# A recurrent kernel whose gaps are filled by hand: 512-column gate groups in even steps, the input product in odd steps, the low-rank layer's products spread out, and the opening in source order

## The chip, the cores and the metric

The kernel runs on one NeuronCore of a Trainium2 chip. The metric is the device time of one execution in microseconds; the kernel before takes 1655.66 us as a median of three runs (1653.91 to 1658.54). One further execution was profiled: it took 1656.13 us, of which the trace shows a span of 1654.2 us from the first instruction to the last.

## What is computed

The input is x of shape 16 x 512 x 512 (batch b, time s, feature) and one condition vector of 512 values for each batch, all fp32. Four residual layers follow one another:

```python
x = x + L0(x, cond)   # L0 comes to x * (1 + gate): gate = sigmoid(silu(cond@W1.T + b1)@W2.T + b2)
x = x + L1(x, cond)   # h_s = tanh(x_s@Wx + b + h_{s-1}@Wh), h_{-1} = cond, 512 steps in a row
x = x + L2(x, cond)   # f, i: sigmoids of x@Wf, x@Wi, divided by f+i+1e-8; candidate x@Wh + b_h;
                      # then a cumulative product and sums along time
x = x + L3(x, cond)   # x @ (base + A_b B_b^T): A_b, B_b of rank 8, made from cond by
                      # LayerNorm, w1, gelu, w2 and a bias
```

Only L1 is a chain through time: step s needs all of step s-1. L2's gates are products of L1's output with three 512 x 512 matrices, and can be formed for any step that is done. L3's factors A_b and B_b depend on the condition alone.

## The kernel before, in words

**Opening (lines 180 to 256).** SP issues the loads in a fixed order: the condition, the vectors, w1, w2, the first block of x, Wx, Wh, the second block. LayerNorm of the condition runs on DVE and is turned on PE (L212). `turned_layer` (L226) forms L0's gate in two products (L231, `ps_hq` and `ps_g`), each with a DVE transpose (L240), a bias (L241) and a sigmoid (L243). `gated` (L164) then makes x1 = x * (gate + 2) of the first two blocks (L166). `begin` (L427) opens a PSUM bank for a later block: ScalarE copies the bias into it (L443), and for the first two blocks PE first writes zeros with small products (L435). In program order these L435 products stand behind `ps_g`, ahead of the first product with Wx.

**The recurrent stage (lines 466 to 548).** 64 blocks of 8 steps. All three kinds of product on PE are cut in four tiles of 32 output partitions, one for each j or c, which run side by side in the array; an fp32 product is two instructions of each kind in the trace. I call four such products side by side of 128 moving columns one *unit*. A step is: 4 units of h @ Wh (L328 with `wh_sb`, 32 instructions); then *filler*, which doesn't depend on this step; then ScalarE's tanh in four parts (L508), DVE's four transposes (L509), whose first result lets PE go on with the next step. In steps 4 to 7 of a block DVE adds the finished pair of steps to x1, giving x2 (L514); in steps 0 to 3 it gates a quarter of the block after next (L166).

The filler is dealt out by hand in program order:
- x1 @ Wx of the next block (`inputs`, L328 with `wx_sb`): 16 units for a block, dealt by `SHARE` (L451 to L454), two to a step as a rule.
- L3's products: one weight chunk of 256 KB gives one unit (`factor_part`, L300), in steps 4 to 7 of blocks 0 to 16. `load_factor` (L281) loads two chunks at once in step 6 and two in step 0 of the next block, into four buffers; factor A comes first (r = 0 to 7), then B with its bias rows (L291). `store_factor` (L309) writes the result to memory. The first of these layers ends in a gelu (L279), in four ScalarE instructions with a table load ahead.
- Part of L2's gates made ahead (`early_gate`, L345): products over 256 columns (L364), equal to two units, one in each of six of eight steps from step 64 and one in every step from step 128. Each gate needs four of them. Of three gates in turn (f, i, candidate) ScalarE makes the sigmoids of f and i (L385), DVE sums them (L406), inverts the sum in four pieces (L388), multiplies (L391, L411, L398), and SP stores the parts (L382). A table `jobs` fixes in which step each piece is emitted; `do_jobs` (L524) comes *ahead of* `begin` (L525 to L529) in a step.

All engines run their own instructions in program order here (manual schedule, L460). PSUM's eight banks are six for the blocks' sums (`ps_r`), one for `pg`, one for `pf`.

**The last stage (lines 553 to 656).** For each batch four `gate_unit`s (L562): three groups of products (L568) over the steps that were not made ahead (from `te`, L564: 128 for batches 0 to 11, 192 for 12 to 15), two sigmoids (L583), a chain of eleven or so DVE instructions (L584 to L599, three scans among them), and two additions on GpSimd (L602, L603) that give x3. `load_layer` (L605) fetches A and B and adds A's bias on GpSimd (L614); `make_layer` (L617) forms base + A B^T on PE (L624) and DVE (L627); `last_layer` (L629) is the product with x3 (L634), a ScalarE copy (L638) and the store. It runs one batch late, after the second gate unit of the next batch; for the last batch after the fourth.

## Time and profile before

| | us |
|---|---|
| median of three runs (lowest, highest) | 1655.66 (1653.91, 1658.54) |
| the profiled execution, its span | 1656.13, 1654.2 |
| first tanh (L508) starts | 21.16 |
| first tanh of block 1, of block 8, of block 17, of block 63 | 37.26, 132.09, 266.25, 911.34 |
| first product of the last stage (L568) starts | 924.12 |
| last_layer of batch 13 has been issued, batch 14's third gate unit starts | 1570.70 |
| the last x3 lets PE go on (L634) | 1637.66 |

The page gives each engine's busy time, and PE is busy almost throughout. Since every product's record overlaps the next, that share says little by itself; what counts is the distance from one start to the next. A row of the timeline is: start, time from the first start to the last end of the merged instructions, engine, line, operation, output and inputs, how many were merged; in brackets the idle time of that engine just before, and what ended it. PEld is the load of the stationary operand, which runs ahead of the product. The granted TensorE clock is 0.999 of full in this execution. DMA is busy for 43% of the time from 37 to 132 us, 40% from 132 to 266 and 13% from 266 to 911. The page lists the queue of PE's instructions with 242 packets and 3.96 MB, and the other instruction queue with 72 and 0.59 MB.

### The profile page before, as it was taken

Reading aid. Unit: us, or ns where it says so; the run is one execution under the profiler, and the core shown is the slowest. Engines: PE = TensorE matmul, PEld = TensorE weight load, DVE = VectorE, ACT = ScalarE, POOL = GpSimd, SP = SyncE. Lnnn points to the kernel's source line nnn. Section 1 sums busy time; section 2 is a strip of 40 time slices with the busy share of each in tenths; the row PEclk is TensorE's granted clock in tenths of the full one; section 3 lists DMA queues with packets and bytes.
Section 4 is the critical chain, followed back from the end, with each engine's and each line's share of the span. In section 5 each row is a group of like instructions: output and inputs, shape, how many; then the busy total and the mean of one; then the engine's idle time right before and its main releaser. Section 6 shows DMA issues by size and latency. Waiting matters only on the chain.

```text
span 1654.2 us, 71063 instructions
## 1 busy us (share of the span) xinstructions
PE 1621.6 (98%) x30885; PEld 1193.3 (72%) x30885; DVE 1126.9 (68%) x3589; ACT 428.3 (26%) x2519; POOL 206.3 (12%) x209
## 2 busy tenths in 40 slices
PE   7999999999999999999999999999999999999997
PEld 6888888888888888888888555555555555556563
DVE  3445555555556556555555789888888888988885
ACT  3333333333333333333333111111111111111111
POOL 0000000000000000000000132232323232323331
PEclk9999999999999999999999999999999999999999
DMA  5444431111111111111110110111111111011111
GB/s 184 115 146 123 132 113 52 36 31 36 36 36 36 36 36 37 36 35 34 36 36 24 24 36 26 40 37 34 41 37 41 37 40 40 27 37 47 47 40 56
DMA packets 109130, 85.76 MB, mean 52 GB/s; under 512 B 23296, under 2 KB 87296, under 8 KB 108816
## 3 DMA queue, kind: packets, MB, share of 16 engines
q1 hardware_dynamic: 107712, 81.12, 16.2%
q8 instruction: 242, 3.96, 1.1%
q14 instruction: 72, 0.59, 0.1%
q10 hardware_dynamic: 1104, 0.08, 0.0%
HBM read 54.43 MB, written 26.74 MB: 49 GB/s over the span
## 4 chain that ended last, share of the span: by engine, by line
PE 94%; DVE 3%; issue 1%; ACT 1%; DMA 1%; SPq 0%; POOLq 0%; POOL 0%; DVEq 0%; ACTq 0%
PE pre L328 41%; PE po L634 12%; PE pg L364 11%; PE pf L568 9%; PE pi L568 9%; PE pc L568 9%; PE pl L624 1%; PE pf L300 1%; DVE s L585 1%; DVE h_out L509 1%; ACT a L508 1%; DVE s L593 0%; DMA w_sb<-in_w1T_dram 0%; DVE s L597 0%; DVE i L596 0%
## 5 line engine op out<-in xcount | busy, mean ns | idle before, releaser
L328 PE MATMUL pre<-wh_sb,h_out 128*32 128x128 f32 x16384 | 553.3, 273 | 8.1 <-issue 2.1
L328 PEld LDWEIGHTS pre<-wh_sb,h_out 128*32 128x32 f32 x16384 | 462.4, 110 | 100.6 <-DVE h_out L509 86.2
L509 DVE STREAM_TRANSPOSE h_out<-a 128x32 f32<-128x32 f32 x2048 | 261.9, 185 | 367.2 <-ACT a L508 366.1
L508 ACT ACTIVATE a<-pre 128x32 f32<-128x32 f32 x2048 | 238.0, 203 | 566.6 <-PE pre L328 564.0
L328 PE MATMUL pre<-wx_sb,x 128*32 128x128 f32 x8192 | 325.4, 273 | 0.7 <-issue 0.7
L328 PEld LDWEIGHTS pre<-wx_sb,x 128*32 128x32 f32 x8192 | 240.3, 110 | 6.6 <-ACT pre L443 5.1
L634 PE MATMUL po<-layer,x 128*128 128x512 f32 x480 | 208.8, 593 | 1.1 <-DVE base_sb L627 1.1
L568 PE MATMUL pf<-x,wf_sb 128*128 128x384 f32 (+1 forms) x512 | 170.6, 476 | 3.5 <-ACT f L583 2.6
L634 PEld LDWEIGHTS po<-layer,x 128*128 128x128 f32 x480 | 91.0, 190 | 113.0 <-issue 106.7
L568 PE MATMUL pi<-x,wi_sb 128*128 128x384 f32 (+1 forms) x512 | 168.8, 473 | 0.0
L568 PE MATMUL pc<-x,wc_sb 128*128 128x384 f32 (+1 forms) x512 | 168.8, 473 | 0.0
L585 DVE RECIPROCAL s<-s 128x384 f32<-128x384 f32 (+1 forms) x64 | 157.0, 2453 | 2.2
L568 PEld LDWEIGHTS pf<-x,wf_sb 128*128 128x128 f32 x512 | 95.8, 190 | 76.8 <-issue 16.6
L568 PEld LDWEIGHTS pc<-x,wc_sb 128*128 128x128 f32 x512 | 97.3, 190 | 61.0
L568 PEld LDWEIGHTS pi<-x,wi_sb 128*128 128x128 f32 x512 | 97.3, 190 | 61.0
L602 POOL TENSOR_TENSOR s<-s,f 128x512 f32<-128x512 f32 x64 | 87.0, 1360 | 386.7 <-DVE s L597 374.5
L514 DVE TENSOR_TENSOR x<-x,h_out 128x128 f32<-128x128 f32 x256 | 101.0, 395 | 26.2 <-PE pg L364 3.7
L556 POOL MEMSET zero<- 128x1 f32 x1 | 0.1, 98 | 924.9 <-DMA early<-ei 924.9
L583 ACT ACTIVATE f<-pf,vec_sb 128x384 f32<-128x384 f32 (+1 forms) x64 | 36.4, 568 | 280.3 <-POOL s L602 134.7
L638 ACT COPY osb<-po 128x512 f32<-128x512 f32 x64 | 37.4, 585 | 267.3 <-PE po L634 149.0
L584 DVE SCALAR_TENSOR_TENSOR s<-f,i 128x384 f32<-128x384 f32 (+1 forms) x64 | 35.5, 555 | 95.3 <-ACT i L583 95.3
L364 PE MATMUL pg<-x,wi_sb 128*32 128x256 f32 x1152 | 90.6, 379 | 1.3 <-ACT ef L385 1.3
(84 smaller groups left out, 1338.1 us busy)
## 6 DMA issues: line engine op xcount, KB each, us to landing
xb<-in_xT_dram SPq DMA_DIRECT2D x64, 256.0 KB
w<-in_l3w_dram SPq DMA_DIRECT2D x64, 256.0 KB
out_dram<-osb SPq DMA_DIRECT2D x64, 256.0 KB
early<-ef SPq DMA_DIRECT2D x36, 128.0 KB
early<-ei SPq DMA_DIRECT2D x36, 128.0 KB
f<-early SPq DMA_DIRECT2D x48, 64.0 KB
i<-early SPq DMA_DIRECT2D x48, 64.0 KB
f<-early SPq DMA_DIRECT2D x16, 96.0 KB
```

The costliest lines, as they stand in the source:

```text
L328: nc.tensor.matmul(pre[PLACE[g][0]][j * BP : (j + 1) * BP, PLACE[g][1], :], lhsT, tile_columns(w, j), start=False, stop=False, skip_group_ ...
L364: nc.tensor.matmul(ps[c * BP : (c + 1) * BP, :, :], w[:, k, j * P + c * BP : j * P + (c + 1) * BP], x2[:, k, batches, steps], start=(k == ...
L508: nc.scalar.activation(a[:, at], pre[bank][:, place, at], AF.Tanh)
L509: nc.vector.transpose(turned[:, c, :], a[:, at])
L514: nc.vector.tensor_tensor(x2[:, :, :, at].rearrange("p k b t -> p k t b"), xs[n][:, :, t0 // 2, :, :], turned.rearrange("p k (t b) -> p k ...
L568: nc.tensor.matmul(p[:, te:], w_sb[:, k, j * P : (j + 1) * P], x2[:, k, b, te:], start=(k == 0), stop=(k == KC - 1),)
L583: nc.scalar.activation(gate[:, new], p[:, new], AF.Sigmoid, bias=col(bias, j))
L584: nc.vector.scalar_tensor_tensor(s[:, new], f[:, new], EPS, i[:, new], ALU.add, ALU.add)
L585: nc.vector.reciprocal(s[:, new], s[:, new])
L602: nc.gpsimd.tensor_tensor(s, s, f, ALU.add)
L634: nc.tensor.matmul(po, x3[:, k, at], layer[:, k, :], start=(k == 0), stop=(k == KC - 1))
L638: nc.scalar.copy(osb, po)
```

## The change

Filler is dealt anew. A gate product covers 512 columns (four units at once), over sets of 4 or 8 batches; it stands in steps 0, 2 and 4 of blocks 8 to 16, and 0, 2, 4 and 6 from block 17. x1 @ Wx takes the odd steps, three or four units in each. There are 18 sets of three gates, with as many gate columns in all as before; batches 0 to 7 have 128 steps made ahead, batches 8 to 15 have 192 for two of the four feature groups and 128 for the others (`made_before`). A set's DVE work is cut into 16 pieces, of which one is done in a step, after the `begin` of that step; the f sigmoid is delayed by six steps. In the last block gates stand in steps 0, 2, 3, 4 and 6.

L3's products stand in steps 1, 3, 5, 7 of blocks 1 to 16. A chunk is loaded whenever one was used, three ahead. B's layers come first; A's bias goes through memory (`turn_bias`, block 2) and is added where the factor is made, with four small loads for each layer, and GpSimd's additions in the last stage go. The gelu is one instruction, its bias added on DVE.

In the opening the zeroing of the banks is done by 24 bf16 products placed ahead of everything else on PE, with the bias copies behind them; the LayerNorm turns stand between the two products of L0; the second and third block of x get buffers of their own. At the end, the last batch's layer is made right after batch 14's gates, and the last gate unit's two additions are done on DVE.

The core of the diff:

```diff
-WIDE = 256
-FIRST, MAIN = 64, 128
-SLOTS = (0, 2, 4, 5, 6, 7)
-QUAD = slice(12, 16)
-PARTS = [(QUAD, slice(0, 64))]
-PARTS += [(slice(b, b + 2), slice(0, 128)) for b in range(0, 12, 2)]
-PARTS += [(QUAD, slice(64, 128)), (QUAD, slice(128, 192))]
+WIDE = 512
+FIRST, MAIN = 64 // T, 128 // T + 1
+SETS = [(slice(8, 16), slice(0, 64), j) for j in (0, 1)]
+SETS += [(slice(b, b + 4), slice(0, 128), j) for b in (0, 4) for j in range(KC)]
+SETS += [(slice(b, b + 4), slice(0, 128), j) for b in (8, 12) for j in (2, 3)]
+SETS += [(slice(b, b + 4), slice(64, 192), j) for b in (8, 12) for j in (0, 1)]
+PARTS = [()] * FIRST + [(0, 2, 4)] * (MAIN - FIRST) + [(0, 2, 4, 6)] * (NBLK - MAIN - 1) + [(0, 2, 3, 4, 6)]
...
+    bias_a = dram.tile([R, D], F32, name="bias_a")
...
+    def begin(n, i, blank=None):
+        bank = ps_r.tile([P, G, P], F32, tag=f"pre{i}", name=f"pre_{n}_{i}")
+        n_place = sum(b == i for b, _ in PLACE)
+        if blank is not None:
+            for j in range(KC):
+                nc.tensor.matmul(
+                    bank[j * BP : (j + 1) * BP, :n_place, :],
+                    blank[:, :BP],
+                    blank[:, : n_place * P].rearrange("p (n f) -> p n f", n=n_place),
+                    start=True,
+                    stop=False,
+                    skip_group_check=True,
+                )
+        nc.scalar.copy(
...
         w1_sb = pre.tile([P, KC, D], F32)
         w2_sb = pre.tile([P, KC, D], F32)
         cond_sb = pre.tile([B, D], F32)
+        nc.sync.dma_start(out=cond_sb, in_=cond)
         nc.sync.dma_start(out=condT_sb, in_=chunks(condT))
-        nc.gpsimd.tensor_copy(h0[:, :, B : 2 * B], condT_sb)
-        nc.sync.dma_start(out=cond_sb, in_=cond)
         nc.sync.dma_start(out=vec_sb, in_=vecs)
         nc.sync.dma_start(out=w1_sb, in_=chunks(w1T))
         nc.sync.dma_start(out=w2_sb, in_=chunks(w2T))
-        x0 = load_x(0, pre)
+        x0 = load_x(0, pre, "x0")
         nc.sync.dma_start(out=wx_sb, in_=chunks(wx))
         nc.sync.dma_start(out=wh_sb, in_=chunks(wh))
-        xb = load_x(1)
+        x1 = load_x(1, pre, "x1")
+        xb = load_x(2)
+        for j in range(KC):
+            nc.scalar.dma_start(
+                out=bias_sb[j * BP : (j + 1) * BP],
+                in_=l1b[:, j * BP : (j + 1) * BP]
+                .rearrange("(o c) f -> o c f", o=1)
+                .to_broadcast([BP, KC, BP]),
+            )
+        blank = pre.tile([P, 2 * P], BF16)
+        nc.gpsimd.memset(blank, 0.0)
+        nc.gpsimd.memset(h0, 0.0)
+        nc.gpsimd.tensor_copy(h0[:, :, B : 2 * B], condT_sb)
         make_identity(nc, ident)
+        for tile_ in (aeT, hT3, b2a_raw, *h_out[G - 2 : T - 1]):
+            nc.gpsimd.memset(tile_, 0.0)
...
-        for k in range(KC):
-            ps = ps_pre.tile([P, B], F32, tag="ae", name=f"ae_{k}")
-            nc.tensor.transpose(ps, xhat[:, k * P : (k + 1) * P], ident[:B, :B])
-            nc.vector.tensor_scalar(
-                aeT[:, k, :B], ps, col(C_LNG, k), col(C_LNB, k), ALU.mult, ALU.add
-            )
-        for j in range(KC):
-            nc.scalar.dma_start(
-                out=bias_sb[j * BP : (j + 1) * BP],
-                in_=l1b[:, j * BP : (j + 1) * BP]
-                .rearrange("(o c) f -> o c f", o=1)
-                .to_broadcast([BP, KC, BP]),
-            )
-        nc.scalar.dma_start(out=b2a_raw[:, :, :R], in_=b2a)
-        def turned_layer(src, w_sb, which, name):
+        banks = [[begin(n, i, blank) for i in range(NBANK)] for n in range(2)]
+        def turned_layer(src, w_sb, which, name, between):
...
+        turned = ps_pre.tile([P, KC, B], F32, tag="ae", name="ae")
+        def turn():
+            for k in range(KC):
+                nc.tensor.transpose(turned[:, k, :], xhat[:, k * P : (k + 1) * P], ident[:B, :B])
+        def scale():
+            for k in range(KC):
+                nc.vector.tensor_scalar(
+                    aeT[:, k, :B], turned[:, k, :], col(C_LNG, k), col(C_LNB, k), ALU.mult, ALU.add
+                )
+        z, gate = turned_layer(lambda k: h0[:, k, B:], w1_sb, C_L0B1, "hq", turn)
         hq = pre.tile([P, KC, BP], F32)
         nc.vector.tensor_tensor(hq, z, gate, ALU.mult)
-        _, gate = turned_layer(lambda k: hq[:, k, :], w2_sb, C_L0B2, "g")
+        _, gate = turned_layer(lambda k: hq[:, k, :], w2_sb, C_L0B2, "g", scale)
...
+    LAYERS = [None] + [(which, r) for which in (1, 0) for r in range(R)]
+    AHEAD = 3
+    chunk_sb = []
+    def load_chunk():
+        m = len(chunk_sb)
+        if m == KC * len(LAYERS):
+            return
+        i, k = divmod(m, KC)
+        w = l3w2[LAYERS[i]] if i else l3w1
+        chunk_sb.append(w2pool.tile([P, D], F32, tag="w2", name=f"w2_{i}_{k}", bufs=AHEAD))
+        nc.sync.dma_start(out=chunk_sb[m], in_=w[k * P : (k + 1) * P, :])
...
+        if k == 0:
+            layer_part.ps = ps_p.tile([P, P], F32, tag="pf", name=f"pf_{i}")
+            if i:
+                which, r = LAYERS[i]
+                layer_part.bias = w2pool.tile([P, P], F32, tag="b2", name=f"b2_{i}", bufs=2)
+                for j in range(KC):
+                    nc.sync.dma_start(
+                        out=layer_part.bias[j * BP : (j + 1) * BP, :],
+                        in_=(bias_a, b2b)[which][r : r + 1, j * P : (j + 1) * P].to_broadcast([BP, P]),
...
+        load_chunk()
+    def end_layer(i):
+        ps = layer_part.ps
         got = w2pool.tile([P, P], F32, tag="got", name=f"got_{i}")
-        if which:
-            nc.vector.tensor_tensor(got, ps, bias, ALU.add)
+        if i:
+            which, r = LAYERS[i]
+            nc.vector.tensor_tensor(got, ps, layer_part.bias, ALU.add)
+            for j in range(KC):
+                nc.sync.dma_start(
+                    out=factor[which][:, r, j * P : (j + 1) * P], in_=got[j * BP : j * BP + B, :]
+                )
         else:
-            nc.vector.tensor_copy(got, ps)
-        for j in range(KC):
-            nc.sync.dma_start(
-                out=factor[which][:, r, j * P : (j + 1) * P], in_=got[j * BP : j * BP + B, :]
-            )
+            z = got.rearrange("p (c f) -> p c f", c=KC)
+            nc.vector.transpose(z, ps.rearrange("p (c f) -> p c f", c=KC))
+            nc.vector.tensor_tensor(z, z, vector_of(C_L3B1), ALU.add)
+            nc.scalar.activation(hT3[:, :, :B], z[:, :, :B], AF.Gelu)
...
+    timed, urgent, pieces = {}, [], []
+    def do_pieces(step):
+        for jobs in (urgent, pieces):
+            if jobs:
+                jobs.pop(0)()
+                break
+        for job in timed.pop(step, ()):
+            job()
...
+        number, which = divmod(u, 3)
+        batches, steps, j = SETS[number]
+        shape = dict(b=batches.stop - batches.start, t=steps.stop - steps.start)
+        first = number < 2
...
+            pool, tag = ((ps_q, "pg"), (ps_p, "pf"))[0 if first else u % 2]
+            early_gate.ps = pool.tile([P, WIDE], F32, tag=tag, name=f"pg_{u}")
...
+        def end_input_gate():
+            sigmoid(i, C_BI)
+            early_gate.sums = [lambda at=at: total(at) for at in halves]
+            pieces.extend(early_gate.sums)
+            for n in range(8):
+                at = slice(n * WIDE // 8, (n + 1) * WIDE // 8)
+                pieces.append(lambda at=at: invert(at))
+            pieces.extend(lambda at=at: normalize(0, at) for at in halves)
         if which == 0:
-            later(now if single else now + 2, lambda: activate(f, AF.Sigmoid, C_BF))
+            timed.setdefault(step if first else step + 6, []).append(lambda: sigmoid(f, C_BF))
         elif which == 1:
-            later(now, lambda: activate(i, AF.Sigmoid, C_BI))
-            later(now + 1, lambda: nc.vector.scalar_tensor_tensor(s, f, EPS, i, ALU.add, ALU.add))
-            for n in range(4):
-                at = slice(n * WIDE // 4, (n + 1) * WIDE // 4)
-                later(now + 2 + n, lambda at=at: part_of_reciprocal(at))
-            later(now + 6, normalize_f)
-            later(now + 7, lambda: nc.vector.tensor_tensor(i, i, s, ALU.mult))
+            timed.setdefault(step, []).append(end_input_gate)
         else:
-            if first:
-                later(now, lambda: activate(candidate, AF.Identity, C_BH))
-            later(now + (3 if first else 4), times_candidate)
...
+            assert not any(job in pieces for job in early_gate.sums)
+            urgent.extend(lambda at=at: times_candidate(at) for at in halves)
...
-    SHARE[0] = (0, 0), (0, 0), (0, 0), (0, 3), (3, 7), (7, 10), (10, 13), (13, 16)
-    for n in range(FIRST // T, MAIN // T):
-        SHARE[n] = (0, 2), (2, 6), (6, 8), (8, 12), (12, 13), (13, 14), (14, 15), (15, 16)
+    SHARE[0] = (0, 0), (0, 0), (0, 0), (0, 3), (3, 5), (5, 7), (7, 9), (9, 11)
+    SHARE[1] = (0, 0), (0, 0), (0, 3), (3, 5), (5, 8), (8, 10), (10, 14), (14, 16)
+    LATE = {0: (11, 14), 1: (14, 16)}
+    for n in range(FIRST, MAIN):
+        SHARE[n] = (0, 0), (0, 3), (0, 0), (3, 6), (0, 0), (6, 9), (9, 13), (13, 16)
+    for n in range(MAIN, NBLK):
+        SHARE[n] = (0, 0), (0, 4), (0, 0), (4, 8), (0, 0), (8, 12), (0, 0), (12, 16)
+    LAYER_STEPS = [(4, 5, 6, 7)] + [(1, 3, 5, 7)] * (len(LAYERS) - 1)
+    LAYER_STEPS += [()] * (NBLK - len(LAYERS))
...
-            step = n * T + s
-            if step >= MAIN or step >= FIRST and s in SLOTS:
-                early_gate.step = step
-                early_gate(made)
+            if s in LAYER_STEPS[n]:
+                layer_part(n, LAYER_STEPS[n].index(s))
+            if s in PARTS[n]:
+                early_gate(made, n * T + s)
...
-            do_jobs(step)
             if s in BEGINS:
                 if s < T - 1 and 0 < n < NBLK - 1:
                     nxt.append(begin(n + 1, BEGINS[s]))
                 elif s == T - 1 and n + 2 < NBLK:
                     ahead.append(begin(n + 2, BEGINS[s]))
-        if n == 0:
-            finish_first(loaded)
-        elif loaded:
-            store_factor(n - 1, loaded)
+            do_pieces(n * T + s)
+        if n < len(LAYERS):
+            end_layer(n)
...
-    for step in sorted(jobs):
-        do_jobs(step)
+            turn_bias()
+        pre, nxt = nxt, ahead
+    while urgent or pieces:
+        do_pieces(S)
...
-        te = TE if b in range(B)[QUAD] else MAIN
+        te = made_before(b, j)
...
-        nc.gpsimd.tensor_tensor(s, s, f, ALU.add)
-        nc.gpsimd.tensor_tensor(x3[:, j, :], s, x2[:, j, b, :], ALU.add)
+        engine = nc.vector if (b, j) == (B - 1, KC - 1) else nc.gpsimd
+        engine.tensor_tensor(s, s, f, ALU.add)
+        engine.tensor_tensor(x3[:, j, :], s, x2[:, j, b, :], ALU.add)
...
-        for c in range(KC):
-            rows = slice(c * BP, c * BP + R)
-            nc.gpsimd.tensor_tensor(at[rows, :], at[rows, :], b2a_sb[rows, :], ALU.add)
...
-            if j == (1 if end else 2):
-                to = base_sb if end else layer
-                make_layer(b, at, bt, to)
-                made = (b, x3, to)
-        pending = made
+            if j == 2 and not end:
+                make_layer(b, *factors, layer)
+            if j == KC - 1 and b == B - 2:
+                make_layer(B - 1, *load_layer(B - 1), base_sb)
+        pending = b, x3, base_sb if end else layer
```

## What I expect, worked out before the run

> **What bounds the kernel now.** I read the page first, then the timeline of single steps, then the start of the first tanh (L508) of each of the 512 steps, whose distances show every disturbance. An undisturbed step comes in two lengths. Past 266 us it is PE's own work:
>
> ```profile
> 302.78 0.62 PE L328 MATMUL pre<-wx_sb,x 128*32 128x128 f32 x16
> 303.03 0.47 ACT L508 ACTIVATE a<-pre 128x32 f32<-128x32 f32 x4 [1.28 <-PE pre L328]
> ...
> 303.22 0.61 PE L364 MATMUL pg<-x,wi_sb 128*32 128x256 f32 x8
> 303.26 0.49 DVE L509 STREAM_TRANSPOSE h_out<-a 128x32 f32<-128x32 f32 x4 [0.71 <-ACT a L508]
> ...
> 303.65 1.06 PE L328 MATMUL pre<-wh_sb,h_out 128*32 128x128 f32 x32
> ```
>
> From start to start: 0.44 us for two units of x1 @ Wx, 0.43 for a gate product, and 0.87 for h @ Wh; a step is 1.742 us. With less filler the chain through ScalarE and DVE sets it:
>
> ```profile
> 40.27 0.62 PE L328 MATMUL pre<-wx_sb,x 128*32 128x128 f32 x16
> 40.52 0.47 ACT L508 ACTIVATE a<-pre 128x32 f32<-128x32 f32 x4 [1.18 <-PE pre L328]
> ...
> 41.02 0.81 PEld L328 LDWEIGHTS pre<-wh_sb,h_out 128*32 128x32 f32 x32 [0.40 <-DVE h_out L509]
> ```
>
> PE waits 0.40 for h; tanh to tanh is 1.644. So up to three units of filler are free, and four cost 1.742. Both schedules deal four units almost everywhere: the gain can come only from what disturbs steps, and from the two ends. Two disturbances stand out.
>
> ```profile
> 307.38 0.47 ACT L385 ACTIVATE ei<-pg,vec_sb 128x256 f32<-128x256 f32 x1 [0.40 <-PE pg L364]
> 307.75 0.38 ACT L443 COPY pre<-bias_sb 128x256 f32<-128x256 f32 x1
> 308.18 0.38 PEld L328 LDWEIGHTS pre<-wx_sb,x 128*32 128x32 f32 x16 [0.27 <-ACT pre L443]
> ```
>
> Every third block a sigmoid that must wait for its product stands ahead of the bank's bias copy, and the next step's x1 @ Wx waits for the copy: that step takes 1.945, 0.20 too long.
>
> ```profile
> 152.51 0.61 PE L328 MATMUL pre<-wh_sb,h_out 128*32 128x128 f32 x15
> ...
> 153.59 0.71 PE L328 MATMUL pre<-wh_sb,h_out 128*32 128x128 f32 x17 [0.47 <-issue]
> ```
>
> Here PE stands still amid h @ Wh, with nothing to wait for. Such gaps lie at the 3542nd, 3925th, 4308th, 4819th, 5203rd, 6225th and 6864th product recorded, 383, 383, 511, 384, 1022 and 639 apart: multiples of 128 but for one or two. 128 products and their loads are 256 instructions, and the page has 242 instruction packets of 16 KB for PE's 61,770. So PE waits for its code. It happens only while DMA is 40% busy (to 266 us).
>
> **The change part by part.** *Opening.* In program order PE zeroes the banks behind the gate's second product:
>
> ```profile
> 15.32 3.67 PE L435 MATMUL pre<-ident,h_out 128*32 128x128 f32 x64 [0.44 <-DVE z_g L240]
> ...
> 18.74 1.43 PE L328 MATMUL pre<-wx_sb,x 128*32 128x128 f32 x32
> ...
> 19.97 1.06 PE L328 MATMUL pre<-wh_sb,h_out 128*32 128x128 f32 x32
> ```
>
> Afterwards the 24 small products run while PE waits for w1 (until 8.47). The first gate product, broken up by the turns (8.47 to 11.58), should take what the second takes (1.98): 1.1 us sooner. From there to the gated x takes 5.5 (11.58 to 17.10), so until 16.0, then 1.23 of x1 @ Wx: h @ Wh at 17.2. Wh must have landed: 4.5 MB up to it, at 268 GB/s (DMA view, first 23 us), takes 16.9, no later. But DVE gates block 1 ahead of the first transposes, and that load landed at 17.94; 0.90 later, at 18.84, the transposes begin. Step 1 then starts at 19.1 instead of 21.73: **2.6** (between 1.5 and 3.2).
>
> *Block 0.* From the second tanh to the ninth took 14.33. Afterwards two steps of four units, five of three: 2 x 1.742 + 5 x 1.644 = 11.7. The gelu made its tanh 1.35 late (table load 1.28, four gelus 0.90). With one gelu (0.24 by the 64-wide shape's nearest row, tanh's 0.20): tanh's end and copy to 0.7, load to 2.0, gelu to 2.2, where 1.64 was due: 0.6 late. **2.0**.
>
> *Blocks 1 to 7* took 94.83 against 56 x 1.644 = 92.06: 2.8 of gaps. Chunks now come one in two steps, not two at once. *Blocks 8 to 16* took 134.16 against 72 x 1.742 = 125.4: 8.7, of which 1.7 is a sigmoid that waits for the store of `ef` (the next use is now eight steps behind the store), 0.65 three steps of five units (none now), 0.9 the copy, and 5.5 gaps. In these blocks the Trainium skill speaks against me: "Runtime: NRT & Kernel Launch", Instruction fetch mechanics, says that code is fetched ahead in 16 KiB blocks and crossing into the next is mostly hidden. By it smoother loads would give nothing, and I would keep 2.8 + 5.5. The gap rows, 0.5 to 0.9 us each, say otherwise. Instructions also fall, from 58 to 55 pairs of load and product a step. Against that stand steps 5 to 7 of blocks 8 to 16, three of 64 pairs in a row. I take 1.6 left of 2.8 and 3.5 of 5.5 (the new table load for sigmoid included): **1.2** (-1 to 2.7) and **5.5** (134.16 - 125.2 - 3.5; 1 to 8.5).
>
> *Blocks 17 to 62* took 645.09. 128 columns take 109 ns and 256 take 216 (1.742 less twelve short ones, halved), so 512 should take 429; two steps are 24 x 0.109 + 2 x 0.429 = 3.478, 1.739 each. The copy now precedes the sigmoid, and its bank is first used a step later. 368 x 1.739 + 0.9 (other gaps, kept) = 640.7: **4.4** (3 to 5.3). The wide sigmoid has no row: 320 and 384 columns take 0.53 and 0.58, so 0.69; twice the 256 would be 0.95. The i sigmoid can start 0.87 after tanh and the next tanh is due at 1.74: cover 0.18, and 0.1 of slack in the chain. At nothing; at most 18 x 0.1. DVE's piece (0.54 at most) ends at 1.80 after tanh where its transposes are due at 1.97. Without that cover each late piece would cost 0.1.
>
> *Last block*: five steps get four units instead of two: 5 x 0.09 = **-0.4**. Nine DVE pieces stand behind the loop instead of five, some 2 us; ScalarE's f in the last stage waited for the last store until 928.14, now until 930.2. PE needs that bank at 931.9: covered.
>
> *SP's queue* gets eight more layers with four bias loads (0.7 each by b2b's row: 2.8 in a 13 us block) and is moved past the x loads; SP waits for DVE over 275 us there, and a chunk is asked for six steps ahead. At nothing; else PE would wait for chunks in odd steps. GpSimd's L614 (35 us) leaves an engine that PE never waits for before 1637.
>
> *Last stage.* PE runs without a gap until batch 13's last layer is done (1570.70). A 384-wide unit costs 1.257 more than a 320-wide ((45.96 - 40.93) / 4, batch to batch). By then 14 narrow units lie behind instead of 10: 5.0 sooner. DVE is the bound after that, without idle time from 1579.23 to 1634.93, then GpSimd:
>
> ```profile
> 1636.35 1.26 POOL L603 TENSOR_TENSOR x<-s,x 128x512 f32<-128x512 f32 x1
> 1637.66 0.50 PEld L634 LDWEIGHTS po<-base_sb,x 128*128 128x128 f32 x2 [4.68 <-POOL x L603]
> ```
>
> Four of its six units become wide, 0.57 each (reciprocal 2.15 to 2.55, the rest 0.17): +2.3. Two additions on DVE (0.69 each) replace 2.66: -1.3. The layer's four additions only change place. So 5.0 - 1.0 = **4.0** (2 to 4.5).
>
> **Sum.** 2.6 + 2.0 + 1.2 + 5.5 + 4.4 - 0.4 + 4.0 = 19.3. The profiled execution (1656.13: span 1654.2 and 1.9 around it) becomes 1636.8; it lay 0.5 above the median, which I leave inside the rounding: **1637**.
>
> **The rivals.** *The code gaps stay* (20%): the three dense steps give as much trouble as the bursts did. The 3.2 won on gaps (1.2 + 2.0) are lost, and the dense run adds 0.3 in each of nine blocks: 1637 + 3.2 + 2.7 = 1643. For it: a step of 64 pairs uses up its 128 instructions in 1.74 us, two of them a packet in 3.5, and packets started 3.4 to 5.2 us apart here. Against: they begin where DMA bursts. *The gaps go entirely* (12%): 1.6 + 3.5 more, 1632. *The change doesn't do what it says* (4%): copies and sigmoids meet elsewhere and the opening stays bound by loads; only the tail and the five-unit steps win: about 1651. *Slower* (4%): four 512-wide products side by side don't run at their columns' rate. Place L364's successor, 432 passes; at 0.50 instead of 0.429 they cost 31 us: 1668. It decides from 0.474 a pass (19.3 / 432 more). Against it: 256 columns cost less than twice 128. *As summed* (60%): 1637.
>
> **How the numbers follow.** The sum's own range is 1633 to 1642. With both gap rivals, 8 in 10 lie between 1631 and 1645. A measurement of this kernel can tell about 0.3%, 5 us: faster by more (under 1650.7) 0.92, within 0.04, slower 0.04.
>
> **What would show it.** First tanh near 18.5 and the ninth near 32.5; two steps together 3.48 past block 17, without a third-block bump; code gaps in blocks 8 to 16 in sum under 3.5; a DVE without idle time at the end and PE going on about 68 us after batch 13's last layer. Wrong would be: gate passes over 0.43, waits for chunks (L332's stationary or moving side) in odd steps, or tanh waiting for a sigmoid.

## The result, and the profile after

The changed kernel takes 1642.02 us (median of six runs, 1639.76 to 1643.44), the kernel before beside it 1656.4: a ratio of 0.991, 95% interval 0.9893 to 0.9927. That is 14 us faster where I had forecast 19: inside the range of 1631 to 1645 that I gave eight chances in ten, and at the upper end of the sum's own range of 1633 to 1642. The profiled execution took 1640.39, its span is 1638.6. From the starts of the tanh and of the last stage's products in the two traces:

| stretch | before | after | gain | forecast |
|---|---|---|---|---|
| to the first tanh of block 1 (opening, block 0) | 37.26 | 34.09 | 3.2 | 2.6 + 2.0 |
| blocks 1 to 7 | 94.84 | 98.19 | -3.4 | 1.2 |
| blocks 8 to 16 | 134.16 | 128.60 | 5.6 | 5.5 |
| blocks 17 to 62 | 645.09 | 640.21 | 4.9 | 4.4 |
| last block, to its last tanh | 11.51 | 11.95 | -0.4 | -0.4 |
| from there to the end of the span | 731.4 | 725.6 | 5.8 | 4.0 |

Three rows are as worked out, three are not. First what came as expected, from the timeline at step 0 of block 20 (start, duration, engine, line, operation):

```profile
302.44 1.04 PE L418 MATMUL pg<-x,wf_sb 128*32 128x512 f32 x8
302.69 0.46 ACT L535 ACTIVATE a<-pre 128x32 f32<-128x32 f32 x4 [0.87 <-PE pre L371]
...
303.30 1.06 PE L371 MATMUL pre<-wh_sb,h_out 128*32 128x128 f32 x32
...
304.17 1.06 PE L371 MATMUL pre<-wx_sb,x 128*32 128x128 f32 x32
304.42 0.47 ACT L535 ACTIVATE a<-pre 128x32 f32<-128x32 f32 x4 [1.10 <-PE pre L371]
...
305.05 1.06 PE L371 MATMUL pre<-wh_sb,h_out 128*32 128x128 f32 x32
```

From 302.44 to 303.30 a gate product of 512 columns takes 0.86, from 304.17 to 305.05 four units of x1 @ Wx 0.88. Wide products run at their columns' rate, which ends the rival on the slower side. Tanh to tanh is 1.73 and 1.75, with no third-block bump.

Now the loss. The timeline at the end of block 2:

```profile
60.22 0.29 DVE L347 TENSOR_TENSOR got<-pf,b 128x128 f32<-128x128 f32 x1
60.54 1.72 SPq L349 DMA_DIRECT2D factor<-got  x4
...
64.97 0.29 DVE L363 COPY b2a_got<-b2a_turned 128x128 f32<-128x128 f32 x1 [4.46 <-DMA factor<-got]
65.18 0.48 DVE L536 STREAM_TRANSPOSE h_out<-a 128x32 f32<-128x32 f32 x4
...
65.44 1.94 PE L371 MATMUL pre<-wh_sb,h_out 128*32 128x128 f32 x32 [4.08 <-DVE h_out L536]
...
67.44 0.47 ACT L535 ACTIVATE a<-pre 128x32 f32<-128x32 f32 x4 [5.82 <-PE pre L371]
```

Read the brackets upward. Tanh waited 5.82 for PE, PE 4.08 for DVE's transposes, and DVE stood 4.46 at L363: `turn_bias` copies into the one buffer tagged `got`, which `end_layer(2)` has just filled and four stores are still reading. DVE works in order, so the transposes of h stand behind a copy whose result nobody needs before block 9. PE also comes back slow: from 65.44 to 67.15 it needs 1.71 for 32 records where 0.87 is normal. Its clock in that stretch (window, its length, PE busy and records, granted clock, DMA share, GB/s):

```profile
65.00:67.00 2.00, 1.56 (x32) 0.50 0.52 193
67.00:69.00 2.00, 2.00 (x60) 0.70 0.08 22
```

In the opening, PE starts the recurrence at the same low rate:

```profile
15.09 1.94 PE L371 MATMUL pre<-wx_sb,x 128*32 128x128 f32 x32 [2.11 <-DVE x L169]
16.77 1.96 PE L371 MATMUL pre<-wh_sb,h_out 128*32 128x128 f32 x32
17.20 0.90 DVE L169 TENSOR_TENSOR x<-xb,g 128x128 f32<-128x128 f32 x4 [2.01 <-DMA xb<-in_xT_dram]
18.48 1.96 PE L371 MATMUL pre<-wx_sb,x 128*32 128x128 f32 x32
```

15.09, 16.77, 18.48: again 1.7 for 32 records. In the kernel before, the 64 zeroing records stood right ahead of the first x1 @ Wx, and the products behind that one came at 0.88.

The end of the last stage. DVE is without a gap until the two additions, and PE waits 1.85 there instead of 4.68:

```profile
1622.14 0.69 DVE L626 TENSOR_TENSOR s<-s,f 128x512 f32<-128x512 f32 x1
1622.87 0.69 DVE L627 TENSOR_TENSOR x<-s,x 128x512 f32<-128x512 f32 x1
1623.61 11.43 PE L655 MATMUL po<-base_sb,x 128*128 128x512 f32 x26 [1.85 <-DVE x L627]
```

### The profile page after: what moved, and what is told of

Read it like the earlier page. It is cut to its first block, busy times and chain, and to the rows that moved or that the text cites. A ratio compares the mean times of both kernels' runs of the same rounds, so it can differ in the third digit from the quotient of the medians.

```text
span 1638.6 us, 67294 instructions
## 1 busy us (share of the span) xinstructions
PE 1610.1 (98%) x29117; PEld 1135.8 (69%) x29117; DVE 1132.8 (69%) x3592; ACT 419.3 (26%) x2476; POOL 173.0 (11%) x144
## 4 chain that ended last, share of the span: by engine, by line
PE 90%; DVE 6%; issue 2%; ACT 1%; DMA 1%; POOL 0%; SPq 0%; DVEq 0%; ACTq 0%; POOLq 0%
PE pre L371 41%; PE po L655 11%; PE pg L418 11%; PE pf L591 8%; PE pi L591 8%; PE pc L591 8%; DVE s L608 1%; PE pl L645 1%; PE pf L332 1%; DVE s L620 1%; DVE s L616 1%; DVE i L619 0%; DVE h_out L536 0%; ACT a L535 0%; DVE f L622 0%
## 5 line engine op out<-in xcount | busy, mean ns | idle before, releaser
L371 PEld LDWEIGHTS pre<-wh_sb,h_out 128*32 128x32 f32 x16384 | 456.4, 110 | 157.8 <-DVE h_out L536 154.7
L371 PE MATMUL pre<-wx_sb,x 128*32 128x128 f32 x8192 | 282.0, 274 | 2.4 <-DVE x L169 2.1
L371 PEld LDWEIGHTS pre<-wx_sb,x 128*32 128x32 f32 x8192 | 233.4, 111 | 3.2 <-issue 3.1
L627 POOL TENSOR_TENSOR x<-s,x 128x512 f32<-128x512 f32 x63 | 83.6, 1328 | 4.9
```

What stands on the lines that cost most here:

```text
L371: nc.tensor.matmul(pre[PLACE[g][0]][j * BP : (j + 1) * BP, PLACE[g][1], :], lhsT, tile_columns(w, j), start=False, stop=False, skip_group_ ...
L627: engine.tensor_tensor(x3[:, j, :], s, x2[:, j, b, :], ALU.add)
```

## Experiments

Each is the changed kernel with one edit; late_chunks and combined join several, and two start from the kernel before and are named so. The kernel before took 1654.4 to 1658.9 beside the different experiments, so each is given as a ratio to it as run on the same chip, and the size of a cause is read from the one execution of each kernel that was traced. I call *code gaps* what tanh-to-tanh distances exceed 1.644 by in blocks 1 to 7 (block 3's pause left out), and 1.742 in blocks 8 to 16 (without bias copies, five-unit steps, waits for stores and the 0.79 of the sigmoid's table load): 0.9 and 2.6 us in the changed kernel, 2.7 and 5.5 in the one before.

**own_tile.** The copy's buffer.

```diff
-        got = w2pool.tile([P, P], F32, tag="got", name="b2a_got")
+        got = w2pool.tile([P, P], F32, tag="b2a_got", name="b2a_got")
```

> The changed kernel, with the turned bias (turn_bias) copied into a tile of its own instead of the shared tile 'got'. My theory: in block 3, step 0, DVE's copy waits 4.5 us for the factor stores that still read 'got', and the transposes of h wait behind it; with its own tile that tanh-to-tanh distance falls from 6.45 us to about 1.7, the next from 2.00 to about 1.75, and all later work comes about 5 us sooner: about 1637 (span 1633.5). Rival: the pause at block 3 is PE's, waiting for its code or for the transpose of the bias; then the 6.45 stays and the time stays at 1642.

1637.12 us, ratio 0.9884 (0.9863 to 0.9906). The first three steps of block 3 take 4.93 instead of 10.10; the timeline there:

```profile
61.63 0.28 DVE L363 COPY b2a_got<-b2a_turned 128x128 f32<-128x128 f32 x1
...
62.42 0.49 DVE L536 STREAM_TRANSPOSE h_out<-a 128x32 f32<-128x32 f32 x4 [0.51 <-ACT a L535]
62.68 1.08 PE L371 MATMUL pre<-wh_sb,h_out 128*32 128x128 f32 x32
```

The copy waits for nothing, and 4.93 is also what these steps took in the kernel before and take in combined. 5.17 us of the forecast went into one shared buffer. Part of that is PE's slow return: in the nine traces with the shared buffer the three steps take 8.39 to 10.12, the least in spread_dense, whose granted clock shows no fall there. The span fell by only 3.7, since in this execution block 1 began 0.5 later (a gap of 0.96 in block 0) and blocks 1 to 7 had 1.8 more of code gaps, while blocks 8 to 16 took 0.8 less.

**warm_pe.** Zero products keep PE busy in the opening.

```diff
+        def warm(groups):
+            for _ in range(groups):
+                for j in range(KC):
+                    nc.tensor.matmul(
+                        banks[1][0][j * BP : (j + 1) * BP, :2, :],
+                        blank[:, :BP],
+                        blank.rearrange("p (n f) -> p n f", n=2),
+                        start=False,
...
                 nc.tensor.transpose(turned[:, k, :], xhat[:, k * P : (k + 1) * P], ident[:B, :B])
+            warm(4)
         def scale():
+            warm(9)
```

> The changed kernel, with 4 groups of four zero products (256 columns, bf16, added to a bank of block 1, so nothing changes) behind the gate's first product and 9 groups behind its second, so that PE is never idle from 7.7 us to the first x1 @ Wx. My theory: in the opening the products run at half rate (32 records in 1.71 us instead of 0.87) because PE had stood idle before them; kept busy, the second gate product and x1 @ Wx take about 0.9 each, the first tanh starts at about 17.1 instead of 18.85, the second at about 19.8 instead of 21.49, and everything later comes about 1.7 us sooner (span 1637). Rival: the opening is bound by its loads (the x of block 1 lands at 17.2, wh shortly before); then the first tanh still moves little, under 0.5 us, and the second with it.

1639.22 us, ratio 0.9889 (0.9873 to 0.9905). The timeline:

```profile
11.53 1.16 PE L257 MATMUL ps_g<-w_sb,hq 128*32 128x128 f32 x32
...
14.76 1.08 PE L385 MATMUL pre<-wx_sb,x 128*32 128x128 f32 x32 [1.08 <-DVE x L169]
18.03 1.46 PE L385 MATMUL pre<-wh_sb,h_out 128*32 128x128 f32 x32 [2.19 <-DMA wh_sb<-in_wh_dram]
```

The first half of my theory holds: the gate's product takes 0.98 from start to start instead of 1.7, x1 @ Wx comes at full rate. But then PE waits for wh until 18.03, and falls back to the low rate: first tanh 19.60, second 22.65. The rival is right about the bound: loads.

**late_chunks.** warm_pe, and L3's first three chunk loads behind the first tanhs, issued by ScalarE.

```diff
-    for _ in range(AHEAD):
-        load_chunk()
...
             do_pieces(n * T + s)
+            if n == 0 and s < AHEAD:
+                load_chunk(nc.scalar)
```

> The changed kernel, with the zero products of warm_pe, and with L3's first three chunk loads (0.75 MB) issued by ScalarE behind the tanh of steps 0, 1 and 2 of block 0 instead of by SP at 10.8 us. Theory: the opening is bound by its loads, and the chunks take bandwidth from wh and from the x of block 1; without them x of block 1 lands at about 16.2 (17.2 in the changed kernel, 18.8 in warm_pe) and wh before, PE stays warm, the first tanh starts at about 17.0 and the second at 18.8, 2.6 us sooner than in the changed kernel (span 1636). Rival: the loads are served in the order of issue, the chunks come last anyway; then wh still lands at 17 to 18, the first tanh starts at 18.5 or later, and the second at 20.5 or later.

1637.96 us, ratio 0.9893 (0.9879 to 0.9908). wh landed at 17.74 and the x of block 1 at 18.47, no sooner than with the chunks ahead, as the rival said: first tanh 18.95. PE went on at full rate (1.80 for step 0), and block 1 began at 33.34, 0.75 to 1.9 sooner than in the changed kernel and the variants so far. But this doesn't show what a warm PE is worth. The second tanh of own_tile, without zero products, and of late_chunks:

```profile
20.63 0.47 ACT L535 ACTIVATE a<-pre 128x32 f32<-128x32 f32 x4 [1.31 <-PE pre L371]
```

```profile
20.75 0.29 ACT L547 ACTIVATE a<-pre 128x32 f32<-128x32 f32 x2 [1.33 <-PE pre L385]
```

Eight traces have the new opening without zero products. In each of them the first x1 @ Wx takes 1.68, but PE reaches its full rate anywhere between 18.2 and 20.9 us, and the second tanh comes between 20.63 and 21.87. Six of the eight then have pauses in block 0 in which PE waited for nothing the trace shows, 0.4 to 1.2 in sum; the changed kernel and tail_undone have none, nor have the three kernels with zero products. With PE busy, the opening is bound by about 4.5 MB of loads; what a warm PE is worth behind them is not shown.

**drain_two.** The pieces left over behind the loop.

```diff
             do_pieces(n * T + s)
+            if n == NBLK - 1:
+                do_pieces(n * T + s)
```

> The changed kernel, with two of the gate pieces on DVE per step in the last block instead of one, so that 2 instead of 9 of them stand behind the loop. My theory of the 2.6 us that PE loses in the first two batches of the last stage (0.37, 0.81 and their like, where the kernel before lost none): ScalarE's first f there waits for the last early stores (until 5.97 us after the stage's first product, before 4.02), DVE starts late, and batch 0's x3 reaches PE late. With the stores sooner, f starts about 3 us after the first product, PE waits for nothing, batch 13's last layer comes 2 us sooner: span about 1636.5. The two pieces fit beside the transposes, so the last block stays at 1.7 a step. Rival: the loss is a matter of DVE's order of work (the reciprocal of the second unit ahead of the scans of the first), not of when it starts; then PE's waits stay within 0.5 us of what they are, and the time stays.

1639.35 us, ratio 0.9889 (0.9874 to 0.9904). ScalarE's first f starts 4.68 after the stage's first product, not 3, but that is enough. PE's waits up to batch 13's last layer, of the changed kernel (from just behind its entry into the stage) and of this one (from the entry on; engine, tile, line, releaser: sum, times, longest):

```profile
PE po L655 <- POOL x L627: 0.8, 1, 0.8
PE pf L591 <- ACT f L606: 0.4, 1, 0.4
```

```profile
PE pf L593 <- DVE x L541: 1.3, 1, 1.3
```

Only the entry into the stage is left. From the first product to batch 0's last layer 47.79 instead of 48.42, from there to batch 1's 45.96 instead of 47.92: the 2.6 us are back. The two waits printed are not all of it: 0.9 is a third pause in the changed kernel, in L645's products, one of whose banks ScalarE had yet to copy out:

```profile
986.28 0.29 PEld L645 LDWEIGHTS pl<-bt,at 8*128 8x128 f32 x2 [0.59 <-ACT osb L659]
```

The edit moved DVE's start (6.05 after the first product instead of 7.05) and put its order of work right at once, so it doesn't separate my theory from the rival.

**before_order.** From the kernel before: the bias copy ahead of the gate job, nothing else.

```diff
-            do_jobs(step)
             if s in BEGINS:
...
+            do_jobs(step)
```

> The kernel before, with one thing of the change alone: the bank's bias copy is issued ahead of the gate job in each step. My theory: this alone removes the third-block bump (1.945 instead of 1.742 in blocks 17 to 62, sixteen times or so) and the like in blocks 8 to 16: 3.2 + 0.9 us less, 1652.3. Rival: the bump is the sigmoid's own length (the wait moves to the tanh of the step instead of the x1 @ Wx behind it), and the time stays at 1656.

1656.17 us beside 1658.89, ratio 0.9984 (0.9976 to 0.9993): 2.7 less, where I had expected 4.1. Blocks 17 to 62 take 641.87 instead of 645.09, 3.22 less, and all sixteen bumps of 0.20 are gone. The timeline shows the two in their new order:

```profile
306.75 0.38 ACT L443 COPY pre<-bias_sb 128x256 f32<-128x256 f32 x1
...
307.12 0.47 ACT L385 ACTIVATE ei<-pg,vec_sb 128x256 f32<-128x256 f32 x1
307.64 0.46 PEld L328 LDWEIGHTS pre<-wx_sb,x 128*32 128x32 f32 x16
307.75 0.62 PE L328 MATMUL pre<-wx_sb,x 128*32 128x128 f32 x16
```

The sigmoid no longer has to wait, and neither has PE. In blocks 8 to 16 the bumps went too, but code gaps were 6.2 there, so nothing is left of it in that stretch.

Five kernels ask what makes the code gaps. **chunks_by_two** brings the bursts of loads back:

```diff
-        load_chunk()
+        if k % 2:
+            load_chunk()
+            load_chunk()
```

> The changed kernel, with L3's chunks loaded two at once after every second product (bursts of 512 KB, as in the kernel before) instead of one after each. The theory of the prediction: PE's code is held up by bursts of loads, so gaps grow: in blocks 1 to 7 (without block 3's pause) from 1.0 to 2.7 us up to 3 or more, in blocks 8 to 16 from 1.7 to 3.4 up to about 5; 3 to 4 us slower than the changed kernel. Rival: only the amount of data or the density of instructions counts; then gaps stay as they are, and the time within 1 us of 1642.

1639.61 us, ratio 0.9908 (0.9892 to 0.9925). Gaps 1.3 and 0.9 us: in sum 2.2 instead of 3.5, not more but fewer. **before_smooth** does the opposite to the kernel before:

```diff
-            if n < 2 * R and s == KC + 2:
-                coming = load_factor(n, None, range(KC // 2))
-            if 0 < n <= 2 * R and s == 0:
-                loaded = load_factor(n - 1, loaded, range(KC // 2, KC))
+            if n < 2 * R and s >= KC + 2:
+                coming = load_factor(n, coming, [s - KC - 2])
+            if 0 < n <= 2 * R and s in (1, 3):
+                loaded = load_factor(n - 1, loaded, [2 + s // 2])
```

> The kernel before, with L3's chunks loaded one at a time (in steps 6, 7, 1 and 3) instead of two in step 6 and two in step 0. In the kernel before and in before_order the code gaps came to 2.7 and 2.3 us in blocks 1 to 7, and to 5.5 and 6.2 in blocks 8 to 16 (without the steps of five units, the wait for a store of ef and the bias copies). The prediction's theory: bursts of loads make them; then they fall to about 1 and 2 (as in the changed kernel), 5 us less: 1650. Rival, which chunks_by_two speaks for: the bursts of chunks do not matter; the gaps stay within 1 us of what they are, and the time at 1655.

1655.01 us, ratio 0.999 (0.9981 to 0.9999). Gaps 1.7 and 4.6, about 1 us less in each stretch than before. My theory asked for 1 and 2; with chunks_by_two beside it, it falls. The 1.7 us wait for a store of `ef` in blocks 8 to 16 is gone here too, without the change.

**gate_halves** raises PE's instructions to what they were (each gate product as two of 256 columns):

```diff
-        for c in range(KC):
-            nc.tensor.matmul(
+        mid = shape["b"] // 2
+        for lo, hi in ((0, mid), (mid, 2 * mid)):
+            for c in range(KC):
+                nc.tensor.matmul(
...
-                x2[:, k, batches, steps],
+                    x2[:, k, batches.start + lo : batches.start + hi, steps],
```

> The changed kernel, with every 512-column gate product issued as two of 256 columns: the same columns, but 16 records in an even step instead of 8, so 58 pairs of load and product a step in blocks 8 to 16 (as in the kernel before) instead of 55. Theory: what shrank the gaps there (5.5 us before, 0.9 to 3.4 without the table load in the changed kernel and its variants) is that gate steps ask PE for less code; with 58 pairs they go back to about 5, and the gaps of blocks 1 to 7 stay. Rival: three pairs a step don't matter, and the gaps stay at 0.9 to 3.4. Of the cost of the columns: 256 columns took 216 ns from start to start, 512 now 429, so blocks 17 to 62 grow by 184 x 4 ns, 0.5 us or so; if wide products were slow, as one rival of the prediction had it, they would shrink.

1642.53 us, ratio 0.9923 (0.9907 to 0.994). Gaps 1.8 and 2.4; three pairs more in a step change nothing that can be seen. Blocks 17 to 62 grow by 0.9.

**spread_dense** breaks up the dense run of steps 5 to 7:

```diff
-        SHARE[n] = (0, 0), (0, 3), (0, 0), (3, 6), (0, 0), (6, 9), (9, 13), (13, 16)
+        SHARE[n] = (0, 0), (0, 3), (3, 6), (0, 0), (6, 9), (9, 13), (0, 0), (13, 16)
...
-PARTS = [()] * FIRST + [(0, 2, 4)] * (MAIN - FIRST) + [(0, 2, 4, 6)] * (NBLK - MAIN - 1) + [(0, 2, 3, 4, 6)]
+PARTS = [()] * FIRST + [(0, 3, 6)] * (MAIN - FIRST) + [(0, 2, 4, 6)] * (NBLK - MAIN - 1) + [(0, 2, 3, 4, 6)]
...
+    for n in range(FIRST, MAIN):
+        LAYER_STEPS[n] = (1, 2, 4, 7)
```

> The changed kernel, with the filler of blocks 8 to 16 dealt so that no three dense steps (64 pairs of load and product) follow one another: gates in steps 0, 3 and 6, L3's products in 1, 2, 4 and 7, x1 @ Wx in 1, 2, 4, 5 and 7; every step keeps its length. Gaps in blocks 8 to 16 (tanh-to-tanh distance above 1.742, without the 0.79 of the sigmoid's table load in block 9) came to 2.6, 1.7, 1.9 and 3.4 us in four executions of the changed kernel and its variants, nearly all in steps 5 to 7. My theory: three dense steps ask for PE code faster than it comes; spread out, the sum falls under 1. Rival: PE's code runs late wherever DMA is busy; then the sum stays between 1.7 and 3.4 and the gaps turn up in other steps.

1642.01 us, ratio 0.992 (0.9901 to 0.9939). Gaps in blocks 8 to 16: 3.5, now in steps 1, 5 and 6. The rival is right.

**no_l3_loads** takes the loads away, with PE's instructions as they are: the first three chunks serve all of L3's layers, so its factors come from the wrong weights.

```diff
+        if m >= AHEAD:
+            chunk_sb.append(chunk_sb[m - AHEAD])
+            return
```

> The changed kernel without the loads of L3's chunks after the first three: the same three tiles serve all 17 layers, so L3's factors are made from the wrong weights, and 17 MB of loads in blocks 0 to 16 are left out. PE's instructions are unchanged. My theory: the gaps need a busy DMA; with it idle but for x and L2's weights they fall under 0.5 us in blocks 10 to 16 and under 1 in blocks 1 to 9 (block 3's pause stays, shorter), the whole gains about 4. Rival: PE's code comes too slowly on its own where instructions are dense; then the gaps of blocks 8 to 16 stay at 1.7 to 3.4.

1637.25 us, ratio 0.9893 (0.9868 to 0.9917). Gaps 0.4 and under 0.1. The rows give window, length, busy time and instructions of PE, PEld, DVE, ACT and POOL, granted clock, DMA share, GB/s. In this kernel DMA is busy for 19% of the window:

```profile
132.00:260.00 128.00, 127.52 (x4016) 109.98 (x4009) 72.75 (x412) 44.50 (x325) 0.00 (x0) 1.00 0.19 51
```

In the changed kernel it is busy for 43%, and PE for 1.4 less:

```profile
132.00:260.00 128.00, 126.09 (x3950) 108.30 (x3944) 71.55 (x404) 43.86 (x320) 0.00 (x0) 1.00 0.43 120
```

But late_chunks has all the loads, DMA busy for 43% as well, and PE as busy as without them:

```profile
132.00:260.00 128.00, 127.52 (x4020) 110.32 (x4014) 72.37 (x410) 44.31 (x325) 0.00 (x0) 1.00 0.43 118
```

Its gaps in blocks 8 to 16 are 0.3, those of combined 0.1. So one execution without the loads doesn't show that gaps need them. Nor does their grouping, three pairs of instructions or the dense run decide, as far as these traces show, how many there are.

**tail_undone.** The last two additions on GpSimd again.

```diff
-        engine = nc.vector if (b, j) == (B - 1, KC - 1) else nc.gpsimd
+        engine = nc.gpsimd
```

> The changed kernel, with the last gate unit's two additions on GpSimd again. The prediction's term: 2.66 on GpSimd for 1.38 on DVE, 1.3 slower. What the trace of the changed kernel suggests beside it: PE paused only 1.85 us before the last products and ran them at full rate from the start (0.43 us from start to start; before, after a pause of 4.68, the first came at 1.01, 0.85, 0.85 and 0.64); by that theory the longer pause brings the slow start back, 1.5 more, so 2.8 in all, and the time from the last x3 to the end of the span goes from 15.0 to 16.5 us. Rival: only the 1.3.

1643.28 us, ratio 0.9934 (0.9913 to 0.9955). From the start of batch 14's last layer until the last x3 let PE go on, 19.54 us instead of 18.32: 1.2 for the additions, as forecast. PE paused 3.07 and still went on at 0.43 a record: the rival is right, the pause alone does not bring the slow start.

**combined.** own_tile, drain_two and late_chunks together.

> The changed kernel with own_tile, drain_two and late_chunks together. If the three causes are separate, their gains add: 4.5 to 5 of block 3, 2.6 of the start of the last stage, 0.5 to 2.6 of the opening, so 8 to 10 less than the changed kernel: 1632 to 1634 (span 1629 to 1631). Rival: what is won is taken back where the next wait ends (DVE in the last stage, the code gaps), and no more than 6 is left: 1636.

1632.94 us, ratio 0.9864 (0.9849 to 0.9879): the interval lies below the changed kernel's, so it beats both kernels. Block 1 begins 0.7 sooner, blocks 1 to 7 take 4.8 less, PE starts batch 13's last layer 2.6 sooner from the last tanh. 2.4 more come from blocks 8 to 16, where this execution had hardly a gap (whether that is chance is open). At the end 1.7 are lost again to a slow start:

```profile
1613.40 13.12 PE L671 MATMUL po<-base_sb,x 128*128 128x512 f32 x26 [2.08 <-DVE x L643]
```

## Why the prediction held, and where it failed

**Blocks 8 to 62: right in size, in part by luck.** No bump, no wait for the store of `ef`, no step of five units, wide products at their rate. My 368 steps of 1.739 and 0.9 of other gaps make 640.9 (I wrote 640.7, so the gain should have read 4.2); it was 640.21, the gaps being 0.1. In blocks 8 to 16 I left 3.5 for gaps and the table load, 2.56 + 0.79 = 3.35 were found; but the ten traces of the changed kernel and its variants with all loads have 0.9 to 4.3 there, so a hit that close is luck. The reason I gave for the smaller gaps, one chunk at a time, is not borne out (chunks_by_two, before_smooth), and that they need DMA traffic is not shown (no_l3_loads, late_chunks). The Trainium skill's "Runtime: NRT & Kernel Launch", Instruction fetch mechanics, has the crossing into the next code block mostly hidden: that fits late_chunks and combined with 0.3 and 0.1 in nine blocks, not the kernel before with 5.5, at about the same share of DMA. Why the changed kernel and its variants with all loads have 0.1 to 3.5 where the kernel before and its variants have 4.6 to 6.2 stays open. The rival in which three dense steps give as much trouble as bursts is not borne out either: breaking them up did not help. That the measured 1642 lies beside that rival's 1643 is a coincidence: the gaps did fall, from 8.2 to 3.5 in blocks 1 to 16, and the loss has another place.

**Blocks 1 to 7: the step that failed.** I costed "*SP's queue* gets eight more layers with four bias loads" at nothing and looked only at SP; for `turn_bias` I did not ask which buffer its copy takes. It took one that stores were reading: 4.5 us on DVE, in order ahead of the transposes, 5.17 in all. Without it these blocks would have gained 1.8 in this execution where I said 1.2; in own_tile, which lacks the wait, they gained nothing (94.79 instead of 94.84), in combined 1.4. The wait is as large as the whole shortfall, 15.6 in the spans and 5.2 making 20.8 against 19.3; the other misses cancel in part.

**Opening: mis-sized.** I summed 2.6 to the second tanh; 1.44 was found (22.93 to 21.49), just under my lower end. I took 1.23 for x1 @ Wx, which is what it took right behind the 64 zeroing records. With the zeroing moved to 1.10 us it took 1.68, and the first h @ Wh 1.71 instead of 0.87. The second of these is partly chance: the same opening has its second tanh between 20.63 and 21.87 in eight traces, so 1.1 to 2.3 sooner than the kernel before. The loads hold PE up where it is kept busy, but wh came at 17.74 to 18.03 in those three traces, not by 16.9. Block 0's 2.0 was 1.7 (14.33 to 12.61): the gelu made its tanh 0.7 late for 0.6, and three of its steps took 1.71, not 1.644. That, too, was one of the two traces of eight without a pause in block 0.

**Last stage: 5.8 for 4.0, four terms off.** The narrow units' 5.0 were there, but 2.6 of it was lost at the start of the stage. I called the nine pieces left behind the loop covered because PE needs that bank only later; true of that bank, but DVE began 7.05 instead of 6.05 after the stage's first product and took the second unit's reciprocal ahead of the first one's scans, so batch 0 came late; drain_two removes both together. The additions gave 1.2 for 1.3. Two gains I had not counted made up for it. At batch 14 ScalarE's sigmoid, and DVE with it, had stood behind a copy that waited for an output store:

```profile
1562.36 0.58 ACT L659 COPY osb<-po 128x512 f32<-128x512 f32 x1 [6.95 <-DMA out_dram<-osb]
1562.84 0.59 ACT L606 ACTIVATE f<-pf,vec_sb 128x384 f32<-128x384 f32 x1
...
1564.06 0.56 DVE L607 SCALAR_TENSOR_TENSOR s<-f,i 128x384 f32<-128x384 f32 x1 [5.69 <-ACT i L606]
```

The copy ends that wait 4.35 after PE began the third gate unit; before, the like of it ended at 1577.69, 6.99 after. DVE's unbroken work therefore began 6.05 instead of 8.53 after that point. I had taken the 8.53 as fixed; that the store came sooner because SP's queue stood differently is argued, not tested. And the last products started at full rate, 1.5 us less. That was chance: see below.

## What to carry to other kernels

When an edit takes a buffer by an old tag, look up who still reads that buffer at that moment: on an engine that works in order, a copy nobody is waiting for can hold up the one chain that matters. When idle-looking work is moved away from the front of a fast stretch, ask whether it kept PE warm, and what bounds the stretch once PE is fast. Where pauses differ between executions of like kernels, take several traces before you put a cause to their number.

## What the hardware showed that I had not expected

The rate of the last products varies between executions. In the kernel before, PE waited 4.68 us and then took 0.85 a record for some 3 us, granted clock 0.50; in before_order it waited as long (4.46 between two starts) and went on at 0.43; in before_smooth it went on at 0.43 for three records and only then fell to 0.85; in combined 2.67 between two starts were enough for the slow rate, in tail_undone 3.66 were not. It hit 3 of 14 traces, each time for 1.5 to 1.7 us. The Trainium skill's "TensorE: Matmul & The Clock Gate", Part 1, describes a window of activity of about 3.4 us that runs freely. The clock records of the traces agree: each of the 12 stretches at 0.50 that end inside a trace lasts 3.41 us, and each stretch at 1.00 between two changes a whole multiple of that, 2 to 478 times. That would explain why the phase, and not the length of a pause alone, decides; no run here varies the phase on purpose. And the granted clock can't be read in the opening: the profile gives 1.00 from 15 to 19 us, while 32 records took 1.7 us there, and 0.50 for the same rate at 65 us. The changed kernel's trace has no clock record before 20.4 us.

Loads of the opening, the same in each kernel, landed up to 1.6 us apart (the x of block 1 at 17.20 in the changed kernel, at 18.82 in warm_pe).
